# Windowed attention with relative position bias: bias products in two column halves of TensorE, spread over the heads by SBUF transfers

## The chip, the cores and the metric

The kernel runs on one NeuronCore of a Trainium2 chip. The metric is the device time of one execution in microseconds. The kernel before takes 4548.22 us, the median of 3 runs (4543.13 to 4551.57). The profile is that of one execution; its span is 4547.9 us.

Engines are called as in the profile: PE is TensorE's matmul, PEld its weight load, DVE is VectorE, ACT is ScalarE, POOL is GpSimd, SP is SyncE, which issues most of the DMAs. L383 is line 383 of the kernel.

## The reference

One layer of a metaformer on x of shape 2 x 128 x 256 x 256 (batch, channels, rows, columns), in float32. It has an attention part and a mixture of experts.

```python
# windows of 8x8 queries; each sees 12x12 keys; 4 heads of 32 channels
qkv = jnp.einsum('bchw,oc->bohw', x, W_qkv)          # x after a norm over channels
attn = jnp.einsum('bnd,bmd->bnm', q, k)              # q scaled
attn = attn + rel_pos_emb(q, rel_height, rel_width) + FIXED_MASK
attn = jax.nn.softmax(attn, axis=-1)
out = jnp.einsum('bnm,bmd->bnd', attn, v)
...                                                   # W_out, residual
# experts: top 2 of 8, on each token
router_probs = jax.nn.softmax(x @ router_w + router_b, axis=-1)
top_p, top_i = jax.lax.top_k(router_probs, K)
expert_out = jnp.einsum('bnd,edc->bnec', x, expert_w) + expert_b
```

`FIXED_MASK` leaves of the keys only those whose row and column differ from the query's by an amount of one parity. So the picture falls apart into four planes by the parity of row and column, and in each a window of 4 x 4 queries sees 6 x 6 keys. `rel_pos_emb` adds to each logit the product of the query with one vector for the difference in rows and one for the difference in columns. With 4 queries and 6 keys in a direction there are 9 possible differences: 18 products of each query and head.

The logits go through a softmax. So a number that is the same for all keys of a query may be added to its logits, and the output stays the same.

## The kernel before

It goes through 256 planes (64 strips of 8 rows, 4 planes each). A plane has 512 queries (4 rows of 128), as 32 windows of 4 columns. While TensorE works on the attention of plane n, it makes the projections of plane n + 1, and the experts' products of a row that an earlier plane has left.

The bias takes these steps. The products of queries and difference vectors are made at once from the normed input, by weights that have both matrices multiplied into each other (`wrel`): 18 rows for each head, in blocks of 32 rows.

```python
NU = 9
...
for h in range(HEADS):
    hp = slice(h * DH, (h + 1) * DH)
    for j in range(2):                      # 0: rows, 1: columns
        c0 = h * DH + NU * j
        nc.vector.tensor_copy(
            relbd[hp, c0 : c0 + NU], relT[j][hp, lo : lo + 2 * NU - 1 : 2]
        )
...
nc.tensor.matmul(pr[:, :P], lhsT=wall[:, 0, :], rhs=relbd, start=True, stop=True)
nc.vector.tensor_copy(wrel, pr[:, :P])
```

```python
def project(n, state):
    ...
    values(0)                               # L368: pvv, 4 products of 128 columns
    yield
    pu = mm_tile(f"pu{n}")
    nc.tensor.matmul(pu, lhsT=wrel, rhs=inner, start=True, stop=True)           # L383
    uT = work.tile([P, PR, 4, 32], F32, tag="uT", name=f"uT{n}", bufs=1)
    nc.vector.transpose(uT, pu.rearrange("p (a m s) -> p a s m", a=PR, s=4))    # L385
    state["shift"] = lambda: shift(uT, n, state)
    yield
    ...                                     # L395 pk (k; one product, two where a batch ends)
    ...                                     # L417 pq (q), then values(4)
```

The transpose (32 x 32 blocks) puts the differences of a query side by side. `shift` then takes, for each query, the 6 of the 9 that its position in the window needs, and transposes back:

```python
def shift(uT, n, state):
    for j in range(2):
        shifted = uT[:, :, :, NU * j + 3 : NU * j + 9]
        dims = [list(d) for d in shifted.ap]
        dims[1 + j][0] -= 1                 # one further on for each query row or column
        nc.vector.tensor_copy(              # L348
            auT[n % 2][:, :, :, 6 * j : 6 * j + 6],
            bass.AP(shifted.tensor, shifted.offset, dims),
        )
    au = work.tile([P, 2 * NP, PR, 4], F32, tag="au", name=f"au{n}")
    nc.vector.transpose(au.rearrange("p m a s -> p a s m"), auT[n % 2])         # L353
    state["au"] = au
```

`au` has, for each head, 12 rows of bias (6 for the rows of keys, 6 for the columns) in the 32 partitions of that head, and a row of -1e30 for keys that a query does not see. A product with 0/1 weights (`keys`) adds them to the logits of all keys:

```python
def scores(n, state):
    qs, kk, au = state["qs"], state["kk"], state["au"]
    ...
    for w in range(2):
        for half in range(2):
            rows = slice(half * SLOT, (half + 1) * SLOT)
            for h in range(HEADS):
                hp = slice(h * DH, (h + 1) * DH)
                nc.tensor.matmul(           # L447, tiles of 32 x 64 of the array
                    sc[rows, h].rearrange("p (t w z) -> p t w z", w=2, z=16)[:, :, w],
                    lhsT=keys[hp, turn, w],
                    rhs=au[hp, half * NP + w : (half + 1) * NP : 2].rearrange(
                        "p t a s -> p t (a s)"
                    ),
                    start=(w == 0),
                    stop=False,
                )
    ...                                     # L464: q by k, 64 products in the same tiles
```

The main loop has its order by hand; what is made on each engine stands in this order (cut):

```python
for n in range(n_planes + 7):
    ...
    if 6 <= n < n_planes:
        nc.tensor.addr_align(BLOCK, offset=BLOCK - FIRST_LIMIT)   # L786; 256, offset 161
    next(score, None)                       # bias and half of q by k
    ...
    next(score, None)                       # the rest; exp of the logits on ACT
    next(ahead, None)                       # pvv
    next(ahead, None)                       # pu
    if n + 1 < n_planes:
        states[n + 1]["shift"]()            # of the plane to come
    next(ahead, None)                       # pk
    next(ahead, None)                       # pq
    ...                                     # pg: gates to a DRAM buffer gd; rb is fetched from it
    ...                                     # four experts' products into acc (L679)
    next(norm, None)                        # squares on ACT (L541)
    next(attn, None)                        # L485 and L495: sums, attention by values
    ...                                     # fetches of gates (gb), on SP's queue; DVE: xe (L670)
    next(norm, None)                        # plt (L547, tiles of 128 x 32), lT on ACT (L555)
    ...
    next(ahead, None)                       # pvv, the other half
    ex.product(0)
    made = next(norm, None)                 # plg (L558)
    ...                                     # experts 1 to 3, po (L523)
```

`addr_align` puts NOPs into TensorE's instruction stream, as many as are needed until the next instruction stands at place 161 of a block of 256.

Of the kernel before, what the change touches and what calls it, by code (L numbers as in the profile page):

```python
# [10 lines left out]
F32 = mybir.dt.float32  # L11
AF = mybir.ActivationFunctionType
ALU = mybir.AluOpType
# [3 lines left out]
P = 128  # L17
HEADS, DH = 4, 32
# [3 lines left out]
NEG = -1e30  # L22
# [16 lines left out]

R = 8
KR, KC = 6, 10
NK = KR * KC
SLOT = 64
BLOCK, FIRST_LIMIT = 256, 95
NU = 9


@with_exitstack  # L50
def kernel(
# [16 lines left out]
    nc = tc.nc  # L68
# [25 lines left out]
    def ctile(shape, name):  # L94
        return const.tile(shape, F32, tag=name, name=name)
# [84 lines left out]
        relT.append(rT)  # L180
    mid = n_rel // 2
    lo = mid - 2 * (PR - 1)
    relbd = ctile([P, P], "relbd")
    nc.gpsimd.memset(relbd, 0.0)
    for h in range(HEADS):
        hp = slice(h * DH, (h + 1) * DH)
        for j in range(2):
            c0 = h * DH + NU * j
            nc.vector.tensor_copy(
                relbd[hp, c0 : c0 + NU], relT[j][hp, lo : lo + 2 * NU - 1 : 2]  # L190
            )
    wrel = ctile([P, P], "wrel")
    pr = mm_tile("p_wrel")
    nc.tensor.matmul(pr[:, :P], lhsT=wall[:, 0, :], rhs=relbd, start=True, stop=True)
    nc.vector.tensor_copy(wrel, pr[:, :P])

    xn, xcol, kcol = [], [], []
    for i in range(2):
# [8 lines left out]
        nc.gpsimd.memset(kcol[i][:, NP - 1, KC - 1 : NK : KC], 0.0)  # L207


    auT = []  # L210
    for i in range(2):
        auT.append(ctile([P, PR, 4, 32], f"auT{i}"))
        nc.gpsimd.memset(auT[i], 0.0)
        nc.gpsimd.memset(auT[i][:, :, :, KR + 6 : KR + 7], NEG)


    def rstd(p4, k0, k1, name):
# [123 lines left out]

    def shift(uT, n, state):

        for j in range(2):
            shifted = uT[:, :, :, NU * j + 3 : NU * j + 9]
            dims = [list(d) for d in shifted.ap]
            dims[1 + j][0] -= 1
            nc.vector.tensor_copy(  # L348
                auT[n % 2][:, :, :, 6 * j : 6 * j + 6],
                bass.AP(shifted.tensor, shifted.offset, dims),  # L350
            )
        au = work.tile([P, 2 * NP, PR, 4], F32, tag="au", name=f"au{n}")
        nc.vector.transpose(au.rearrange("p m a s -> p a s m"), auT[n % 2])  # L353
        state["au"] = au

    def project(n, state):

# [22 lines left out]


        pu = mm_tile(f"pu{n}")
        nc.tensor.matmul(pu, lhsT=wrel, rhs=inner, start=True, stop=True)  # L383
        uT = work.tile([P, PR, 4, 32], F32, tag="uT", name=f"uT{n}", bufs=1)
        nc.vector.transpose(uT, pu.rearrange("p (a m s) -> p a s m", a=PR, s=4))  # L385
        state["shift"] = lambda: shift(uT, n, state)
        yield

# [46 lines left out]
    def scores(n, state):  # L435


        qs, kk, au = state["qs"], state["kk"], state["au"]
        turn = place(n // 4, 0) // 2
        att = ps_att.tile([P, 4, 512], F32, tag="att", name=f"att{n}")  # L440
        sc = att[:, :, 0:HQ]
# [3 lines that stand above are left out]
                for h in range(HEADS):  # L445
                    hp = slice(h * DH, (h + 1) * DH)
                    nc.tensor.matmul(  # L447
                        sc[rows, h].rearrange("p (t w z) -> p t w z", w=2, z=16)[:, :, w],
                        lhsT=keys[hp, turn, w],
                        rhs=au[hp, half * NP + w : (half + 1) * NP : 2].rearrange(  # L450
                            "p t a s -> p t (a s)"
                        ),
                        start=(w == 0),
                        stop=False,
                    )
# [287 lines left out]
    for _ in project(0, states[0]):  # L743
        pass
    states[0]["shift"]()
    if n_planes > 1:
        columns(1)

# [22 lines left out]
    with tc.manual_schedule(engines={ET.PE, ET.DVE, ET.Activation, ET.Pool, ET.SP}):  # L771
        for n in range(n_planes + 7):
# [43 lines left out]
            if f or c:  # L816
                norm = norms(f, c, f"_{n}")
            next(norm, None)
            next(attn, None)
            nxt.means()  # L820
            new.fetch_means()
# [97 lines left out]
```

The softmax here doesn't subtract the row's maximum and nothing guards it: scores larger than these inputs give would overflow.

## Time and profile before

| | before |
|---|---|
| time, median of 3 runs | 4548.22 us |
| PE busy | 4490.6 us, 99% of the span |
| DVE busy | 3826.1 us, 84% |
| ACT busy | 1582.6 us, 35% |
| POOL busy | 1321.7 us, 29% |
| DMA | 824.84 MB, 181 GB/s |
| granted TensorE clock | 0.997 |

A group of instructions in the profile is a line of the kernel with an engine, an operation, and what it writes and reads: `L385 DVE STREAM_TRANSPOSE uT<-pu`. Behind it stand the count, the busy time of all in us, and the mean of one in ns. A tile of the array stands before the shape: `128*32` is 128 rows by 32 columns. Each fp32 product shows as two MATMUL records, its two passes. Matmuls are pipelined and their ends are modelled, so the distance between starts says more of them than the durations. "issue" is idle time in which the engine waited for nothing that the profile shows. The chain of work that ended last is followed back from the last instruction, at each step to what released it.

### The profile page before, as it was taken

How to read it: one execution, taken by the hardware profiler on the slowest of the kernel's cores; microseconds unless marked ns; L12 is line 12 of the kernel's file. 1: busy time of each engine (PE TensorE's matmuls, PEld its weight loads, DVE VectorE, ACT ScalarE, POOL GpSimd, SP SyncE). 2: the span in 40 equal slices, each digit the busy share in tenths (PEclk: the TensorE clock that was granted, in tenths of full speed). 3: DMA queues.
4: the chain of work that ended last, by engine and by line, in shares of the span. 5: the costliest groups of instructions: out<-in, count | busy, mean ns of one | idle time of the engine just before them, and what ended most of it. 6: DMA issues, size and time to landing. Idle time of an engine off the chain costs nothing.

```text
span 4547.9 us, 224166 instructions
## 1 busy us (share of the span) xinstructions
PE 4490.6 (99%) x96841; PEld 2708.2 (60%) x96841; DVE 3826.1 (84%) x11330; ACT 1582.6 (35%) x4542; POOL 1321.7 (29%) x1812
## 2 busy tenths in 40 slices
PE   7999999999999999999999999999999999999997
PEld 5665666565666666666666666666666656656653
DVE  5888888888888888888888888888888888888886
ACT  3333333333333333333333333333333333333331
POOL 1232323232323223232323232323232323232221
PEclk9999999999999999999999999999999999999999
DMA  2565666566556666665656665656666656666655
GB/s 76 176 191 180 190 179 191 181 190 180 189 180 189 183 186 184 186 185 183 188 181 186 183 188 181 190 180 190 180 190 180 191 179 190 182 187 181 188 163 181
DMA packets 457786, 824.84 MB, mean 181 GB/s; under 512 B 52480, under 2 KB 64356, under 8 KB 456804
## 3 DMA queue, kind: packets, MB, share of 16 engines
q1 hardware_dynamic: 456074, 810.21, 59.0%
q8 instruction: 769, 12.60, 1.1%
q14 instruction: 213, 1.74, 0.1%
q10 hardware_dynamic: 730, 0.29, 0.0%
HBM read 737.95 MB, written 72.34 MB: 178 GB/s over the span
## 4 chain that ended last, share of the span: by engine, by line
PE 97%; DVE 1%; issue 1%; DMA 0%; ACT 0%; POOL 0%; SPq 0%; ACTq 0%; DVEq 0%; POOLq 0%
PE acc L679 38%; PE pvv L368 12%; PE att L464 7%; PE att L495 6%; PE plt L547 6%; PE pu L383 5%; PE po L523 5%; PE pk L395 5%; PE pq L417 5%; PE att L447 3%; PE att L485 3%; PE pg L622 1%; PE plg L558 1%; DMA gb<-gd 0%; DVE xe L670 0%
## 5 line engine op out<-in xcount | busy, mean ns | idle before, releaser
L679 PE MATMUL acc<-xe,ew 128*128 128x512 f32 x4096 | 1921.7, 595 | 6.5 <-DVE xt L685 2.6
L679 PEld LDWEIGHTS acc<-xe,ew 128*128 128x128 f32 x4096 | 720.8, 191 | 788.1 <-issue 780.3
L670 DVE TENSOR_TENSOR xe<-xs,gb 128x512 f32<-128x512 f32 x1536 | 950.5, 686 | 10.9 <-DMA gb<-gd 2.2
L674 POOL COPY last<-xe 128x1 f32<-128x1 f32 x256 | 48.3, 189 | 3110.8 <-DVE gb L653 3103.7
L670 POOL TENSOR_TENSOR xe<-xs,gb 128x512 f32<-128x512 f32 x512 | 652.3, 1275 | 5.7 <-PE att L495 2.7
L368 PE MATMUL pvv<-wt,xcol 128*128 128x128 f32 x4096 | 595.1, 288 | 4.2 <-POOL xcol L330 3.1
L368 PEld LDWEIGHTS pvv<-wt,xcol 128*128 128x128 f32 x4096 | 497.2, 191 | 66.6 <-issue 51.9
L555 ACT COPY lT<-plt 128x128 f32<-128x128 f32 x260 | 69.3, 266 | 1141.3 <-PE plt L547 1141.3
L271 POOL TENSOR_TENSOR xn<-xt,rb 128x512 f32<-128x512 f32 x249 | 375.9, 1510 | 79.9 <-DMA rb<-gd 68.1
L464 PE MATMUL att<-qs,kcol 32*64 32x32 f32 x32768 | 391.7, 226 | 2.4 <-issue 2.4
L464 PEld LDWEIGHTS att<-qs,kcol 32*64 32x64 f32 x32768 | 390.3, 130 | 2.6 <-issue 2.6
L375 ACT COPY vv<-pvv 128x512 f32<-128x512 f32 x512 | 300.3, 586 | 207.4 <-PE pvv L368 191.4
L495 PEld LDWEIGHTS att<-pT,vv 64*32 64x32 f32 x32768 | 347.8, 105 | 36.7
L472 ACT ACTIVATE pT<-att 128x1024 f32<-128x1024 f32 x256 | 262.1, 1024 | 253.7 <-PE att L464 250.3
L495 PE MATMUL att<-pT,vv 64*32 64x32 f32 x32768 | 342.5, 200 | 0.0
L385 DVE STREAM_TRANSPOSE uT<-pu 128x512 f32<-128x512 f32 x256 | 183.5, 717 | 150.2 <-PE pu L383 150.2
L541 ACT ACTIVATE sq<-xt 128x512 f32<-128x512 f32 x505 | 292.1, 628 | 0.0
L353 DVE STREAM_TRANSPOSE au<-auT 128x512 f32<-128x512 f32 x256 | 269.2, 1051 | 9.0
L406 ACT COPY kcol<-pk 128x560 f32<-128x560 f32 (+2 forms) x344 | 174.3, 507 | 268.5 <-PE pk L395 265.7
L523 PE MATMUL po<-o,wt 128*128 128x512 f32 x512 | 261.8, 593 | 4.1 <-DVE r__0_619 L227 1.0
L383 PE MATMUL pu<-xn,wrel 128*128 128x512 f32 x512 | 263.6, 596 | 0.0
L417 PE MATMUL pq<-xn,wt 128*128 128x512 f32 x512 | 262.2, 593 | 0.5 <-issue 0.2
(2700 smaller groups left out, 5579.8 us busy)
## 6 DMA issues: line engine op xcount, KB each, us to landing
gb<-gd SPq DMA_DIRECT2D x2048, 256.0 KB
xt<-in_x_dram SPq DMA_DIRECT2D x256, 256.0 KB
sb<-gd SPq DMA_DIRECT2D x256, 256.0 KB
out_dram<-xt SPq DMA_DIRECT2D x256, 256.0 KB
rb<-gd SPq DMA_DIRECT2D x249, 256.0 KB
gd<-gT SPq DMA_DIRECT2D x245, 20.0 KB
ew<-in_L_ffn_expert_w_dram SPq DMA_DIRECT2D x1, 512.0 KB
eb<-in_L_ffn_expert_b_dram SPq DMA_DIRECT2D x1, 512.0 KB
```

The source lines that it names most:

```text
L271: eng.tensor_tensor(xn[i % 2][:, :, :, k, 1 : PC + 1], ln1_src(i, k).rearrange("p (y j x) -> p y x j", y=2, x=2), rb.rearrange("p (y j x) ...
L368: nc.tensor.matmul(pv[:, t * P : (t + 1) * P], lhsT=xl[:, t0 + t].rearrange("p a k -> p (a k)"), rhs=wv, start=True, stop=True,)
L375: nc.scalar.copy(vv[:, t0 : t0 + 4, :].rearrange("p t c -> p (t c)"), pv)
L383: nc.tensor.matmul(pu, lhsT=wrel, rhs=inner, start=True, stop=True)
L417: nc.tensor.matmul(pq, lhsT=wq, rhs=inner, start=True, stop=True)
L464: nc.tensor.matmul(sc[rows, h, 32 * t : 32 * t + 32], lhsT=kk[hp, half * HP + t, :], rhs=qs[hp, m0 : m0 + 2].rearrange("p m a s -> p (m a ...
L495: nc.tensor.matmul(av[hp, half, 32 * t : 32 * t + 32], lhsT=vv[rows, t, hp], rhs=pT[rows, h, 32 * t : 32 * t + 32], start=True, stop=True,)
L523: nc.tensor.matmul(po, lhsT=wo, rhs=state["o"].rearrange("p f z -> p (f z)"), start=True, stop=True)
L541: nc.scalar.activation(sq, src, AF.Square)
L547: nc.tensor.matmul(plt[32 * t : 32 * t + 32, :P], lhsT=rw[:, j], rhs=src[:, t * P : (t + 1) * P], start=(j == srcs[0][0]), stop=(j == srcs ...
L670: eng.tensor_tensor(self.xe[e], self.xs, self.gb.pop(e), ALU.mult)
L679: nc.tensor.matmul(self.acc, lhsT=ew[:, e, :], rhs=self.xe.pop(e), start=(e == 0), stop=not self.xe)
```

## The change

It makes the bias rows with 16 differences for each head in place of 18. The last of the 9 differences of a direction is subtracted from the other 8; that is the same number for all keys of a query, so the softmax does not see it, and the ninth difference becomes zero. Four heads of 16 rows fill 64 rows, half of the array's columns. So the plane's 512 queries are taken in two halves of 256, and each half has its own 64 columns of the array and its own 64 partitions of the result. Both products are meant to run at once. The transposes of DVE then have 256 elements in each partition in place of 512.

What comes out of DVE (`both`) has the four heads at 16 partitions each, twice. The product that adds the bias to the logits needs each head at the 32 partitions of that head. Eight transfers from SBUF to SBUF, issued by ACT, bring them there (`send`), into two buffers `au` that planes use in turn.

```diff
-    relbd = ctile([P, P], "relbd")
+    relbd = ctile([P, HEADS * NB], "relbd")          # NB = 16
...
-            c0 = h * DH + NU * j
-            nc.vector.tensor_copy(
-                relbd[hp, c0 : c0 + NU], relT[j][hp, lo : lo + 2 * NU - 1 : 2]
+            c0 = h * NB + (NU - 1) * j
+            last_d = lo + 2 * (NU - 1)
+            nc.vector.tensor_tensor(
+                relbd[hp, c0 : c0 + NU - 1],
+                relT[j][hp, lo : last_d - 1 : 2],
+                relT[j][hp, last_d : last_d + 1].broadcast_to([DH, NU - 1]),
+                ALU.subtract,
             )
...
     def shift(uT, n, state):
-        for j in range(2):
-            ...
-        au = work.tile([P, 2 * NP, PR, 4], F32, tag="au", name=f"au{n}")
-        nc.vector.transpose(au.rearrange("p m a s -> p a s m"), auT[n % 2])
-        state["au"] = au
+        to = auT[n % 2]
+        for up, (rows, start) in enumerate(((slice(0, 64), 3), (slice(64, P), 1))):
+            ...                                       # 64 partitions x 96 elements
+            nc.vector.tensor_copy(...)
+        src = uT[:, :, :, NU + 2 : NU + 8]
+        for h in range(2):
+            ...                                       # 128 partitions x 48 elements
+            nc.vector.tensor_copy(...)
+        nc.vector.memset(to[0:64, 0, :, :, 5:6], 0.0)
+        nc.vector.memset(to[:, :, 0, :, 11:12], 0.0)
+        both = work.tile([P, 2 * NP, 8], F32, tag="both", name=f"both{n}")
+        nc.vector.transpose(
+            both.rearrange("p m (a s) -> p a s m", a=2), to.rearrange("p a s h k -> p a s (h k)")
+        )
+        state["both"] = both
+
+    def send(n, state):
+        both = state.pop("both")
+        for up in range(2):
+            for h in range(HEADS):
+                r = (up * HEADS + h) * NB
+                nc.scalar.dma_start(au[n % 2][h * DH : h * DH + NB, up], both[r : r + NB])
...
         pu = mm_tile(f"pu{n}")
-        nc.tensor.matmul(pu, lhsT=wrel, rhs=inner, start=True, stop=True)
-        uT = work.tile([P, PR, 4, 32], F32, tag="uT", name=f"uT{n}", bufs=1)
-        nc.vector.transpose(uT, pu.rearrange("p (a m s) -> p a s m", a=PR, s=4))
+        for up in range(2):
+            nc.tensor.matmul(
+                pu[up * 64 : (up + 1) * 64, 0 : NQ // 2],
+                lhsT=wrel,
+                rhs=inner[:, 2 * up : 2 * up + 2],
+                start=True,
+                stop=True,
+            )
+        uT = work.tile([P, 2, 4, 32], F32, tag="uT", name=f"uT{n}", bufs=1)
+        nc.vector.transpose(uT, pu[:, 0 : NQ // 2].rearrange("p (a m s) -> p a s m", a=2, s=4))
...
-                        sc[rows, h].rearrange("p (t w z) -> p t w z", w=2, z=16)[:, :, w],
+                        sc[rows, h].rearrange("p (t w a z) -> p t w a z", w=2, a=2, z=8)[:, :, w],
                         lhsT=keys[hp, turn, w],
-                        rhs=au[hp, half * NP + w : (half + 1) * NP : 2].rearrange(
-                            "p t a s -> p t (a s)"
+                        rhs=bias[hp, :, half * NP + w : (half + 1) * NP : 2].rearrange(
+                            "p a t z -> p t a z"
                         ),
...
             next(norm, None)                          # the squares on ACT
+            if n + 1 < n_planes:
+                send(n + 1, states[n + 1])
             next(attn, None)
```

The alignment of TensorE's instructions (`BLOCK`, `FIRST_LIMIT`) stays as it was.

## The prediction

> **What bounds the kernel now.** I read the page first: the busy times, then the chain that ended last.
>
> ```profile
> PE 4490.6 (99%) x96841; PEld 2708.2 (60%) x96841; DVE 3826.1 (84%) x11330; ACT 1582.6 (35%) x4542; POOL 1321.7 (29%) x1812
> ...
> PE 97%; DVE 1%; issue 1%; DMA 0%; ACT 0%; POOL 0%; SPq 0%; ACTq 0%; DVEq 0%; POOLq 0%
> ```
>
> TensorE is busy 99% of the span and 97% of the chain is TensorE. A busy PE alone proves little, so I then read one plane of the steady part in the chain in order of time (start, length, what):
>
> ```profile
> 2011.35 0.86 PE po L523 x2
> 2012.21 0.86 PE acc L679 x2
> 2013.07 0.60 PE att L447 x30
> 2013.67 1.34 PE att L464 x80
> 2015.01 1.09 PE pvv L368 x8
> 2016.10 0.86 PE pu L383 x2
> 2016.96 0.86 PE pk L395 x2
> ```
>
> The pieces touch: no other engine is in the chain. The same piece (pk) begins at 1999.57 and at 2016.96, so a plane takes 17.39 us, and 256 planes give 4452 of the 4548 us. A microsecond of TensorE work taken from a plane is therefore worth close to a microsecond; a microsecond of DVE work is worth almost nothing. pu is one piece of 0.86 us, in two passes (x2), one for each half of the fp32 product.
>
> **What the Trainium skill says.** (1) TensorEngine Tiling (Array Packing), Key Properties: tiles of the array work in parallel, but changing the tiling mode drains TensorE. The trace agrees with both, and has the size. In the timeline of TensorE (start, us from first start to last end):
>
> ```profile
> 2006.49 0.43 PE L547 MATMUL plt<-xt,rw 128*32 128x128 f32 x8
> 2006.73 0.40 PE L547 MATMUL plt<-sq,rw 128*32 128x128 f32 x8
> 2006.95 0.40 PE L547 MATMUL plt<-xt,rw 128*32 128x128 f32 x8
> 2007.17 0.40 PE L547 MATMUL plt<-sq,rw 128*32 128x128 f32 x8
> ```
>
> Eight passes of 128 columns in four column tiles begin every 0.22 us, so 0.11 us for four tiles at once: the tiles do run together, although the two passes of one product follow each other in the program. The last eight should end streaming at 7.17 + 0.22 = 7.39, but the next piece, full-width pvv, starts at 7.50: 0.11 us of drain. Its first pass to second takes 0.21 us in the record against 0.11 for each later one: another 0.10 us, the weight load that nothing hides after a drain. Into tiles it is cheaper: the last full acc pass begins at 2012.48, streams 0.43 and ends at 2012.91, and L447 begins at 2013.00, 0.09 later; and its first group of passes takes about 0.04 longer than the rest (0.153 against 0.109).
> (2) DMA: Bandwidth & Descriptors, Anatomy of one DMA: about 2 us are fixed, mostly the receipt of the last byte. Here the 20 KB transfer gd is issued at 2019.78 and rb, which waits for it, at 2021.08: 1.3 us, to be used instead.
> (3) Runtime: NRT & Kernel Launch, Instruction fetch mechanics: instructions are fetched in blocks of 256. This kernel aligns its TensorE stream to such blocks once per plane, and the trace shows the padding as NOPs.
> (4) TensorE: Matmul & The Clock Gate, Part 1: an idle window of some 3.4 us halves the clock. No steady plane here is idle so long; it matters below.
>
> **The change part by part.**
>
> *pu.* Before, from the start of the last pvv pass to the second pass of pk: 0.112 (pvv streams) + 0.432 + 0.432 (pu) + 0.428 (pk) = 1.404 us. After, pu has two tiles of 128x64, each two passes of 256 columns. Side by side a pass is 0.215. But full-width pvv stands before it and full-width pk behind it, so there are two mode changes that were not there: 0.112 + 0.093 (drain) = 0.205; first pass 0.215 + 0.043 = 0.258; second pass and drain 0.215 + 0.113 = 0.328; first pk pass 0.428 + 0.101 = 0.529. Sum 1.320. The saving is 0.084 us, not the 0.43 that half the columns promise. Times 256: -21.5 us.
>
> *DVE.* The costs before:
>
> ```profile
> L385 DVE STREAM_TRANSPOSE uT<-pu 128x512 f32<-128x512 f32 x256 | 183.5, 717 | 150.2 <-PE pu L383 150.2
> ...
> L353 DVE STREAM_TRANSPOSE au<-auT 128x512 f32<-128x512 f32 x256 | 269.2, 1051 | 9.0
> ```
>
> Both transposes halve: about 0.38 and 0.54 us instead of 0.72 and 1.05. Two copies of 96 elements stay (0.17 each), two of 48 and two tiny memsets come (about 0.4 together). Net about -0.45 us a plane. DVE is not on the chain: 0.
>
> *The eight transfers.* In each plane ACT issues eight DMAs of 16 KB (16 rows of 1 KB). At the start of the program ACT's issues follow each other at 0.5 us (0.77, 1.26, 1.79), so eight hold its queue some 4 us. They are placed behind the two squares (last end 2003.12), and the next ACT instruction there is
>
> ```profile
> 2007.64 0.27 ACT L555 COPY lT<-plt 128x128 f32<-128x128 f32 x1 [4.52 <-PE plt L547]
> ```
>
> ACT is idle for 4.52 us before it: the issues just fit. What depends on lT, plg, comes at 2009.36 on TensorE, so lT may slip by over 1 us before TensorE waits. The last rows land some 2 us after the last issue, at about 2010, and L447 reads them at 2013.07. 128 KB more per plane against 3.2 MB (181 GB/s by 17.39 us) is 4% more traffic at 59% load. So in the steady part: hidden. Two leaks: the DMA issues of SP and ACT use eight completion semaphores in turn, so the eighth send waits until rb has landed; in the 26 planes where POOL waits for a late rb (68.1 us, of which 28.9 in one), lT may come half a microsecond too late: +5. And planes 0 to 5 take 12 to 14 us instead of 17.39 (no experts yet), so there landing after the issue is late by 1 or 2 us each: +8.
>
> *The padding.* A plane has 756 TensorE passes and loads (2 x 96841 / 256), three semaphore waits and nine NOPs: 768, three blocks. In four planes where the batch ends (k is made in two products) there are four NOPs. The padding rows, over 2234 to 2300 us and in one ordinary plane:
>
> ```profile
> L786 PEldq NOP  x16: 13/13/13, 2235.1 to 2289.2; - x16
> ```
> ```profile
> L786 PEldq NOP  x9: 13/13/13, 2411.4 to 2411.9; - x9
> ```
>
> The change adds four instructions (a second product: two loads, two passes) and waits: each head's first bias product must await two landings. One wait rides on an instruction, the other is an instruction of its own; four heads, four more. 763 + 4 = 767: ordinary planes still fit, with one NOP. The four planes at the batch's end had room for four, need eight, and are padded to 1024: 252 NOPs. A NOP looks cheap (13 ns), but 74 of them at plane 6 ran from 108.2 to 113.6 us, 0.073 us each. 252 take 18.4 us. TensorE has about 3.7 us of queued work when the padding begins (from the wait for o, about 2026.6, to L447 at 2030.39), so it stands some 14.5 us, four times: 58; with a cold clock for a while after each, 65 us.
>
> Sum: 4548 - 21.5 + 8 + 5 + 65 = 4604; I say 4600.
>
> **The rivals.** *No padding accident* (the waits count otherwise, or k's planes fit): 4548 - 21 + 13 = 4540. For it: the change leaves the alignment as it was, and my tally rests on how many waits the eight landings need. *The waits need more than five instructions:* then every plane pads to 1024 and stands 14 us, above 8000 us. Against it: a product already waits for one earlier reader, and the tally of 767 leaves one over. *Halves one after the other:* pu gains nothing and pays both mode changes, 0.35 us a plane, +88 instead of -21. Against it: plt's four tiles overlap. *The mode change is cheap for two halves:* up to 0.43 x 256 = -110, 4440. Against it: both kinds of switch show the drain. *ACT becomes the wait:* if an issue takes 0.8 us instead of 0.5, lT slips 2 us and TensorE waits about 1 us a plane, +250. Against it: the transfers have 16 rows each, fewer than those at the start.
>
> **Range and chances.** The padding accident has about 0.75 by my count, and centres on 4600; without it 4540. Eight in ten: 4530 to 4645. Faster by over 2% (below 4457) needs the drains to vanish: 0.03. Slower by over 2% (above 4639) needs serial halves, a blocked ACT or padding everywhere: 0.18. Within 2%: 0.79.
>
> **What would show it.** pu as 128*64, 128x256, four records a plane, two starts within 0.01 us; about 0.2 us of idle in all around pu; pk's first pass longer by 0.1; the plane at 17.30 us. DVE busy lower by about 110 us. ACT's eight issues between the squares and lT, lT still just after plt. Four planes near 2235 to 2310 with some 250 NOPs and 30 us each, all others with one. I am wrong if planes 128 to 131 are as long as others, if the steady plane is not shorter by 0.05 to 0.12 us, or if L447 waits for a landing in the steady part.

## The result and the profile after

A plane is counted from its first bias product (L447 before, L488 after) to that of the next one. An ordinary plane is one from 6 to 247 outside the four at the batch's end. A bracket behind a ratio is its 95% interval.

| | before | after |
|---|---|---|
| time, median | 4546.16 us | 4919.62 us (4916.77 to 4928.26) |
| ratio | | 1.0823 [1.0805, 1.0842] |
| ordinary plane, median | 17.405 us | 18.585 us |
| ordinary plane, mean | 17.429 us | 18.559 us |
| start to the first L447 or L488 | 31.54 us | 33.19 us |
| planes 0 to 5 together | 82.14 us | 100.69 us |
| four planes at the batch's end | 71.6 us | 141.4 us |
| from plane 248 on | 214.7 us | 223.4 us |

The change costs 8.2% where 1% was predicted. The rows add up: 238 ordinary planes by 1.13 us (mean) are 269, the four planes 70, the start 1.7 + 18.6, the end 9, together 368 us; the two profiled spans differ by 4916.3 - 4547.9 = 368.4 us. The four planes were in the prediction. The 1.13 us in every ordinary plane was not.

The page of the changed kernel, busy times and chain by engine:

```profile
PE 4603.8 (94%) x97353; PEld 2739.2 (56%) x97353; DVE 3695.0 (75%) x12354; ACT 1580.1 (32%) x4542; POOL 1330.3 (27%) x1814
...
PE 92%; issue 6%; DVE 1%; DMA 1%; ACTq 1%; ACT 0%; POOL 0%; SPq 0%; DVEq 0%; POOLq 0%
```

TensorE still makes the chain, but 6% of it is now "issue": TensorE stood and waited for nothing that the profile names. And PE's busy time rose by 113 us although the change takes work from it. Both have to be found. The chain in order of time (start, length, what), one plane:

```profile
2010.62 0.61 PE att L488 x30
2011.23 1.34 PE att L505 x80
2012.57 1.09 PE pvv L402 x8
2013.65 0.58 PE pu L418 x4
2014.24 0.63 PE pk L436
2014.87 0.45 issue
2015.31 0.70 PE pk L436
...
2020.99 1.49 PE att L536 x78
...
2023.49 1.09 PE pvv L402 x8
...
2028.98 0.60 PE att L488 x30
```

Two pieces differ from the plane of before. pk is cut in two with a hole between its passes, and the product of probabilities and values (L536, before L495; called the dense block below) takes 1.49 us; before it began at 2005.22 and the product after it at 2006.49. Over all planes, from start to start, the second pass of pk comes 1482 ns after the first (median; before 428), and the 128 passes of L536 take 1384 ns from first to last (before 1145). With pu and the weight load it shows, the way from the last pvv pass to the second pass of pk is 0.205 + 0.274 + 0.309 + 1.482 = 2.270 us against 1.404, +0.87; L536 has +0.24; together 1.11 of the 1.13.

The groups of the changed kernel (busy in us, mean ns of one, idle before and what ended it) that answer to those shown of before:

```profile
L488 PE MATMUL att<-au,keys 32*64 32x128 f32 x8192 | 184.0, 284 | 63.5 <-issue 60.9 <-DMA au<-both 2.4
...
L377 DVE STREAM_TRANSPOSE both<-auT 128x256 f32<-128x256 f32 x256 | 164.7, 643 | 27.2 <-DVE auT L375 8.2
L426 DVE STREAM_TRANSPOSE uT<-pu 128x256 f32<-128x256 f32 x256 | 115.2, 450 | 166.2 <-PE pu L418 166.2
...
L599 PE MATMUL plg<-ident,lT 128*128 128x128 f32 x260 | 71.4, 275 | 13.5 <-ACT lT L596 13.5
```

The last of them in the kernel before:

```profile
L558 PE MATMUL plg<-ident,lT 128*128 128x128 f32 x260 | 70.9, 273 | 0.0
```

The transposes have shrunk from 717 to 450 and from 1051 to 643 ns. TensorE waited 2.4 us in the whole run for a landing in au, and 13.5 us for lT (before none), all of it in planes 0 to 5. So in the steady part hardly anything waits for the transfers. They hurt in another way, below.

### The profile page after: what moved, and what is told of

It is laid out like the page before. It is cut to its first block, busy times and chain, and to the rows that moved or that the text cites. A ratio compares the mean times of both kernels' runs of the same rounds, so it can differ in the third digit from the quotient of the medians.

```text
span 4916.3 us, 228790 instructions
## 1 busy us (share of the span) xinstructions
PE 4603.8 (94%) x97353; PEld 2739.2 (56%) x97353; DVE 3695.0 (75%) x12354; ACT 1580.1 (32%) x4542; POOL 1330.3 (27%) x1814
## 4 chain that ended last, share of the span: by engine, by line
PE 92%; issue 6%; DVE 1%; DMA 1%; ACTq 1%; ACT 0%; POOL 0%; SPq 0%; DVEq 0%; POOLq 0%
PE acc L720 35%; PE pvv L402 11%; PE att L505 7%; PE att L536 7%; PE pk L436 7%; PE plt L588 5%; PE po L564 4%; PE pq L458 4%; PE att L488 3%; PE pu L418 3%; PE att L526 3%; PE pg L663 1%; PE plg L599 1%; ACTq L388 1%; DMA gb<-gd 0%
## 5 line engine op out<-in xcount | busy, mean ns | idle before, releaser
L436 PE MATMUL pk<-xn,wt 128*128 128x512 f32 (+2 forms) x528 | 356.2, 684 | 186.7 <-issue 186.7
L546 DVE STREAM_TRANSPOSE sT<-att 128x512 f32<-128x512 f32 x256 | 183.5, 717 | 377.8 <-PE att L536 377.8
L536 PEld LDWEIGHTS att<-pT,vv 64*32 64x32 f32 x32768 | 394.7, 105 | 52.7 <-issue 3.2
L536 PE MATMUL att<-pT,vv 64*32 64x32 f32 x32768 | 402.7, 200 | 2.9 <-issue 2.8
L505 PE MATMUL att<-qs,kcol 32*64 32x32 f32 x32768 | 397.0, 227 | 6.5 <-issue 6.5
L505 PEld LDWEIGHTS att<-qs,kcol 32*64 32x64 f32 x32768 | 395.8, 131 | 6.9 <-issue 6.9
L447 ACT COPY kcol<-pk 128x560 f32<-128x560 f32 (+2 forms) x344 | 174.1, 506 | 506.2 <-PE pk L436 502.5
L436 PEld LDWEIGHTS pk<-xn,wt 128*128 128x128 f32 x528 | 98.7, 189 | 415.4 <-issue 320.9
L569 DVE TENSOR_TENSOR xt<-po,xt 128x512 f32<-128x512 f32 x256 | 177.1, 692 | 125.1 <-PE po L564 125.0
L628 ACT ACTIVATE lg<-lg 128x32 f32<-128x32 f32 x256 | 58.7, 229 | 659.2 <-DVE lg L627 659.2
```

Source lines behind the costliest of these rows:

```text
L436: nc.tensor.matmul(pk[:, : m * PC], lhsT=wk, rhs=xp[:, part[0] : part[0] + m, 1 : PC + 1], start=True, stop=True,)
L505: nc.tensor.matmul(sc[rows, h, 32 * t : 32 * t + 32], lhsT=kk[hp, half * HP + t, :], rhs=qs[hp, m0 : m0 + 2].rearrange("p m a s -> p (m a ...
L536: nc.tensor.matmul(av[hp, half, 32 * t : 32 * t + 32], lhsT=vv[rows, t, hp], rhs=pT[rows, h, 32 * t : 32 * t + 32], start=True, stop=True,)
```

## The experiments

The base of a run is the kernel before or the changed kernel; an edit stands on its own. A few fixes stay in as the series goes on, and each says from which run it starts. Times are medians; the kernel before was timed beside each group, at 4543 to 4550 us.

### 1. Where the end of an instruction block falls

The prediction counted how many instructions a plane has, and not which instruction stands at a block's end. In the compiled stream of TensorE, counted, the end of the second block of a plane falls before instruction 351. In the kernel before that is the first of the expert products (acc), with pu, pk, pq and pg in front of it. In the changed kernel the plane has eight more instructions by there (four waits in L488, four for pu), and number 351 is the weight load of pk's second pass. The Trainium skill, Runtime: NRT & Kernel Launch, Instruction fetch mechanics, says that crossing to the next block is "mostly hidden". Two runs move the block's end alone.

b_fl87, the kernel before with its block's end moved eight instructions, onto pk:

```diff
-BLOCK, FIRST_LIMIT = 256, 95
+BLOCK, FIRST_LIMIT = 256, 87
```

> The kernel before with nothing changed but the place of its TensorE instructions in the fetch blocks: 8 slots on, so that a block ends between the two passes of pk, where it ends in the changed kernel. Theory (the block's end costs the time): pk's second pass starts about 1.4 us after its first instead of 0.43, L495 takes some 0.2 us longer, the plane goes from 17.40 to about 18.5 us and the whole to about 4830 us. Rival (the time comes from the transfers, ACT or the tiling mode): nothing of that is in this kernel, so it stays at 4546 us.

Measured: 4764.72 us, ratio 1.0486 [1.047, 1.0502]: nothing of the change is in this kernel, and it loses 219 us. The chain:

```profile
2019.67 0.86 PE pu L383 x2
2020.54 0.43 PE pk L395
2020.96 0.89 issue
2021.85 0.70 PE pk L395
2022.55 0.86 PE pq L417 x2
```

The hole stands where it stands after, between the two passes of pk; from pass to pass it is 1288 ns (median). Here the crossing is not hidden. L495 kept its 1146 ns: the part of the expectation that had the second loss from the block's end as well is refuted.

a_fl103, the changed kernel with the block's end back before acc:

```diff
-BLOCK, FIRST_LIMIT = 256, 95
+BLOCK, FIRST_LIMIT = 256, 103
```

> The changed kernel with the alignment moved by 8 slots, so that the blocks end before the same instructions as in the kernel before (the first of the experts' products, and the 208th of L536). Theory: the steady plane falls from 18.58 to 17.31 us (the 0.084 us of pu gained), the four padded planes (66 us) and the first planes (20 us) stay, the whole is about 4612 us. Rival: still about 4900 us.

Measured: 4698.17 us, 1.0332 [1.0317, 1.0348]; a plane takes 17.654 us.

```profile
2026.66 0.58 PE pu L418 x4
2027.24 1.06 PE pk L436 x2
2028.30 0.86 PE pq L458 x2
```

pk is one piece again, 534 ns from pass to pass, which is the 0.529 of the prediction. Of the 1.13 us a plane, the block's end is thus 0.95 (1482 - 534 ns), the largest term of the whole result. But the total stayed 86 us above what was expected, as L536 did not recover: 1482 ns. So L536 has a cause of its own.

The traces also have the fetches: packets of 16 KB on the DMA queue q8, three a plane. Of each ordinary plane, the first of them, and what follows it (medians in us, the lowest in brackets):

| run | fetch starts after the plane's start | second pass of pk after the fetch's start | first acc after the fetch's start |
|---|---|---|---|
| before | 2.87 | 1.36 | 2.76 (2.20) |
| a_fl103 | 2.84 | 1.31 | 2.71 (2.20) |
| after | 2.75 | **2.35** (2.17) | 3.85 |
| b_fl87 | 2.74 | **2.36** (2.17) | 3.86 |

The change does not move the fetch. Where pk's second pass stands first in the new block, it comes some 2.35 us after the fetch's start and never under 2.17, although the time from pass to pass goes from 0.9 to 1.9 us in nine planes of ten (after). By the work alone it would come 1.3 us after it, and acc 2.7. That this fetch brings the block that is waited for is inferred from these times.

### 2. The four padded planes

a_fix: from a_fl103, the alignment is left out for planes 128 to 131. The limits are set so that the blocks end before acc in the planes after these; in planes 6 to 127 they end sixteen instructions later, behind the first eight acc passes.

```diff
-BLOCK, FIRST_LIMIT = 256, 95
+BLOCK, FIRST_LIMIT = 256, 119
...
-            if 6 <= n < n_planes:
-                nc.tensor.addr_align(BLOCK, offset=BLOCK - FIRST_LIMIT)
+            if 6 <= n < n_planes and not 128 <= n < 132:
+                limit = FIRST_LIMIT if n < 128 else FIRST_LIMIT - 16
+                nc.tensor.addr_align(BLOCK, offset=BLOCK - limit)
```

> As a_fl103, but around the end of the batch the alignment is left out for four planes, and the places before and after differ by the 16 slots that those planes add, so no plane is padded to a fourth block. Theory: the four planes lose their 15 to 17 us each: about 4546 us, 66 us below a_fl103. If the padding is not what holds them, no difference.

Measured: 4636.4 us, 1.0198 [1.0183, 1.0213]; the four planes take 17.8 to 17.9 us each, 69 us less together than in a_fl103. The total fell by 62 us only, because the new limit pads elsewhere: 254 NOPs stand ahead of plane 6, from 130.7 to 149.5 us, where a_fl103 has 14, and planes 0 to 5 take 115.9 us in place of 98.9. In the changed kernel the rows of the padding (count, first and last start) show the ordinary planes with one NOP, 18.6 us apart, and one of the four with its many:

```profile
L828 PEldq NOP  x2: 13/13/13, 2211.2 to 2229.8; - x2
```
```profile
L828 PEldq NOP  x206: 13/13/13, 2400.0 to 2415.2; - x103
```

and its chain shows what they cost, 12.87 us of issue before L488:

```profile
2402.48 12.87 issue
2415.35 1.27 PE att L488 x22
```

In the 14.65 us behind it the granted clock was 0.84, and the products took longer (L488 1.27 us in place of 0.61).

### 3. The second loss: what slows L536

nosend_fl99: the changed kernel without its eight transfers, block's end before acc. The scores then lack nearly all of the bias.

```diff
-BLOCK, FIRST_LIMIT = 256, 95
+BLOCK, FIRST_LIMIT = 256, 99
...
-                nc.scalar.dma_start(au[n % 2][h * DH : h * DH + NB, up], both[r : r + NB])
+                pass
```

> As a_fl103, but the eight transfers are left out, so the bias is missing from the logits and the output is not the reference's; TensorE loses four waits, so the alignment is set to bring the blocks' ends to the same instructions. Theory (the transfers are hidden in the steady part): the plane is the same as in a_fl103 within 0.05 us; the four planes fit their three blocks again and the first planes lose the wait, so about 4525 us. Rival (the transfers hold ACT or the DMA queues): the steady plane is shorter than that of a_fl103 by 0.2 us or more.

Measured: 4522.4 us, 0.995 [0.9934, 0.9967]; L536 1145 ns, a plane 17.304 us. The rest of the change brings what the prediction gave it: 17.405 - 0.084 = 17.32. The transfers cost some 0.33 us a plane (a_fix against this run), and 0.31 of it lies in L536.

Within L536 of a_fl103 the loss is not spread. From pass to pass TensorE keeps its pace, with single stops in between, mostly of 75 to 180 ns. Of 396 stops over 60 ns in 245 planes (one of 0.11 us near the block's start, which the kernel before has too, is not counted), 386 begin 150 to 300 ns after an issue of a transfer by ACT began. The issues follow each other every 0.64 us, so this does not tell the start of one from the end of the one before. Is it the bytes, the time, or the place in the stream?

a_fix2_tiny: from a_fix, 32 bytes of each row in place of 1 KB (most of the bias is left out).

```diff
-                nc.scalar.dma_start(au[n % 2][h * DH : h * DH + NB, up], both[r : r + NB])
+                nc.scalar.dma_start(au[n % 2][h * DH : h * DH + NB, up, 0:1], both[r : r + NB, 0:1])
```

> Block ends as in the run a_fix (4636 us, L536 from first to last start 1455 ns); each of the 64 rows-by-halves transfers of a plane stays, but carries 8 elements of a row (32 bytes) in place of 256 (1 KB), so 4 KB a plane in place of 128 KB; most of the bias is left out, so the output is not the reference's. If the bytes that the transfers move through SBUF slow L536: L536 back to about 1150 ns and the total about 4560 us. If it is the eight issues, their descriptors and their semaphores: L536 stays at 1350 to 1480 ns and the total is 4610 to 4640 us. Waits of lT for the transfers get shorter in both cases and bring nothing to the total.

Measured: 4637.5 us, 1.0192 [1.0177, 1.0207], L536 1469 ns, as a_fix. A transfer of 512 bytes stops TensorE as long as one of 16 KB. It isn't the bytes; the number of rows, 16, was the same. (The expectation's count of 64 transfers a plane is a slip: it is eight.)

a_fix2_late: from a_fix, `send` is called after `lT` and the next load of x, and the scores read the other buffer (the bias of another plane).

```diff
-        qs, kk, bias = state["qs"], state["kk"], au[n % 2]
+        qs, kk, bias = state["qs"], state["kk"], au[(n + 1) % 2]
...
-            if n + 1 < n_planes:
-                send(n + 1, states[n + 1])
             next(attn, None)
...
             load_x((n + 9) // 4, (n + 9) % 4, paced=True)
+            if n + 1 < n_planes:
+                send(n + 1, states[n + 1])
```

> Block ends as in the run a_fix; the eight sends are issued by ScalarE after the probability transposes of the plane instead of before L536, and the scores read the other bias buffer, so that nothing waits for them sooner than they land (the bias of another plane is added, so the output is not the reference's). If L536 is slow only because the sends run beside it: L536 at about 1150 ns and, with nothing else slowed, a plane of 17.30 us and a total of about 4550 us. If any sends of the plane slow whatever TensorE does meanwhile: the 0.3 us turns up in another block (L488 or the gate's matmuls) and the total stays at 4620 to 4640 us. If L536 is slow from its place in the stream and not from the sends: L536 stays at 1455 ns.

Measured: 5167.65 us, 1.1356 [1.1336, 1.1375]. L536 is at 1145 ns, so the time at which the transfers run decides. But the gain is more than lost elsewhere, which no theory had. From the waits (us in total, times, longest):

```profile
ACT vv L409 <- DMA au<-both: 1712.9, 253, 9.8
```

There ACT stands at its issues for 6.8 us a plane, and the copies of vv, kcol and qs behind them are late for TensorE.

a_fix2_pufirst: from a_fix, pu is made before the first pvv, directly behind L505, which works in parts of the array too. Then one change of mode is saved.

```diff
-        values(0)
-        yield
         pu = mm_tile(f"pu{n}")
...
         state["shift"] = lambda: shift(uT, n, state)
         yield
+        values(0)
+        yield
```

> Block ends as in a_fix; pu is made before the first pvv instead of after it, so the two-halves products stand behind other matmuls that also use part of the array, and one change of mode with its weight load in the open (205 ns from pvv to pu in the changed kernel) is saved; the sends come about 1 us sooner. If the drain is saved: 0.1 to 0.2 us a plane, total 4590 to 4615 us, L536 unchanged at about 1450 ns or a little shorter. If the change of mode costs the same in the new place: within 5 us of a_fix's 4636 us. If the earlier sends leave L536 in part: below 4580 us.

Measured: 4585.53 us, 1.0081 [1.0064, 1.0097]; a plane takes 17.475 us, 0.157 less than in a_fix (medians; 0.126 in the mean), L536 1455 ns. Another 18 us came in planes 0 to 5 and the start: 2 NOPs stand ahead of plane 6 in place of a_fix's 254. Without that the total would lie in the range expected.

a_fix2_split: from a_fix2_pufirst, four of the eight issues go to SP, directly after the copies.

```diff
                 states[n + 1]["shift"]()
+                send(n + 1, states[n + 1], (0,), nc.sync)
...
-                send(n + 1, states[n + 1])
+                send(n + 1, states[n + 1], (1,))
```

> As a_fix2_pufirst, but the four transfers of the first half are issued by SyncE directly after the copies, and only four are left to ScalarE at the old place. If the sends slow L536 by running beside it: fewer run beside it, L536 falls to 1150 to 1300 ns and the total to 4500 to 4570 us. If the number of transfers or their bytes in a plane counts and not when they run: the total stays within 10 us of a_fix2_pufirst. Against both: SyncE's four issues may hold back the loads that it issues next, and then the waits of L488 for its experts' inputs would grow.

Measured: 4805.83 us, 1.0565 [1.0549, 1.0581]. L536 (here L534) is at 1358 ns, but the point named against both came true: SP's four issues took 3.15 us (median), its load of the gate's rows began 11.9 us after the plane's start in place of 7.9, and the work on the normalised x came late, and pq with it. From the waits:

```profile
POOL xn L284 <- DMA rb<-gd: 744.5, 243, 37.8
PEld pq L456 <- DVE uT L421: 369.4, 242, 2.4
```

### 4. The disputed cost by itself

Four runs on the kernel before, each with eight transfers a plane of 16 rows by 512 bytes that nobody reads, at the place where the change has its `send`. Only the two ends and the issuing queue differ.

```diff
             next(norm, None)
+            for up in range(2):                                        # b_sends
+                for h in range(HEADS):
+                    r = (up * HEADS + h) * 16
+                    nc.scalar.dma_start(dump[n % 2][h * DH : h * DH + 16, up], ident[r : r + 16])
```

b_dram reads `c_keys[r : r + 16, 0]` in DRAM in place of `ident`; b_sp has `nc.sync` in place of `nc.scalar`; b_store writes 16 rows of `ident` to a tile in DRAM.

> The kernel before, unchanged but for eight transfers a plane that nobody reads: ScalarE issues, at the place where the changed kernel has its sends, eight copies of 16 rows of 512 bytes of a constant tile into a scratch tile. PE's stream stays at 759 instructions. If each issue by ScalarE that falls beside L495 stops TensorE for 0.10 to 0.17 us, about two a plane: L495 from 1145 ns to 1400 to 1480 ns, nothing else of TensorE changed, a plane from 17.40 to 17.65 to 17.75 us, total 4605 to 4630 us. If L536's slowing came from anything else of the change (the place of the block's end, waits for au or both, the order of work on VectorE): L495 stays at 1145 ns and the total within 10 us of 4546 us.

> As b_sends (4631 us, L497 1428 ns, 1.7 stalls a plane), but the eight unread transfers take their 512-byte rows from DRAM instead of SBUF; ScalarE issues them at the same place. If ScalarE's issue beside the dense block is what stops TensorE: L497 again 1380 to 1460 ns and the total 4610 to 4640 us. If it is the reading of SBUF by transfers: L497 at 1145 ns and the total at 4540 to 4560 us.

> As b_sends, but SyncE issues the eight unread transfers from SBUF, at the same place of the program. If any queue's transfers from SBUF to SBUF stop TensorE: L497 at 1300 to 1460 ns, with stalls that begin 150 to 300 ns after an issue by SyncE. If only ScalarE's issues do: L497 at 1145 ns, no stalls. The total tells little here, as SyncE's loads of the experts' gates stand behind the eight: 4560 to 4800 us in either case.

> As b_sends (4631 us, L497 1428 ns) and b_dram (4560 us, 1145 ns), but the eight unread transfers, 16 rows of 512 bytes each, go from SBUF to DRAM. If the reading of SBUF is what stops TensorE: the dense block at 1300 to 1460 ns and the total 4590 to 4635 us. If it takes a transfer from SBUF to SBUF: the block at 1145 ns and the total at 4540 to 4565 us.

| run | from, to, issued by | time, us | ratio | dense block, ns |
|---|---|---|---|---|
| b_sends | SBUF to SBUF, ACT | 4630.88 | 1.0199 [1.0183, 1.0215] | 1428 |
| b_sp | SBUF to SBUF, SP | 4969.32 | 1.0928 [1.091, 1.0946] | 1474 |
| b_dram | DRAM to SBUF, ACT | 4560.38 | 1.0032 [1.0019, 1.0045] | 1145 |
| b_store | SBUF to DRAM, ACT | 4571.81 | 1.0045 [1.0028, 1.0061] | 1146 |

b_sends repeats the second loss without anything else of the change: 0.28 us in each plane's dense block against 0.31 in a_fix. (That both totals are 2.0% above is chance: a_fix also has the gain of pu and the padding ahead of plane 6.) Its timeline (start, length, what), the issues of ACT and the dense block (the product of L495):

```profile
2028.51 3.81 ACTq L824 DMA_DIRECT2D dump<-ident  x6
...
2030.75 1.67 PE L497 MATMUL att<-pT,vv 64*32 64x32 f32 x128
```

The same in b_dram:

```profile
2028.11 2.32 ACTq L824 DMA_DIRECT2D dump<-in_c_keys_dram  x5
...
2029.47 1.34 PE L497 MATMUL att<-pT,vv 64*32 64x32 f32 x128
```

In both, issues run on beside the block; only in b_sends is the block longer. It isn't the issue by ACT, as the block of b_sp is slow too. And it isn't the reading of SBUF alone, as b_store is not slow: the first theory of b_dram's expectation and of b_store's falls, and what is left is a transfer with both ends in SBUF. The dose shows it plane by plane. Counted in planes 10 to 254 are the transfers whose issue ended inside the block, up to 0.28 us before its last pass starts, and beside them the block's median length in ns (planes in brackets; three planes of gap4 with three transfers are left out):

| run | 0 | 1 | 2 |
|---|---|---|---|
| b_sends | | 1301 (78) | 1484 (167) |
| b_sp | | 1309 (68) | 1502 (177) |
| a_fix2_tiny | | 1306 (64) | 1492 (181) |
| gap4 (below) | 1145 (117) | 1331 (104) | 1510 (21) |
| b_dram | | 1145 (58) | 1145 (187) |
| b_store | 1146 (2) | 1146 (59) | 1146 (184) |

A transfer from SBUF to SBUF costs the block 0.16 to 0.19 us, a second one as much again; to or from DRAM nothing. Why TensorE stops is not shown. The Trainium skill, SBUF — State Buffer, SBUF: two separate sides, says that accesses of engines and of transfers to SBUF do not get in each other's way; b_dram and b_store agree; the stops of b_sends do not fit it, unless they come about outside SBUF, which no run here tells.

The total of b_sp is above its range, and most of it is something else, a hole before acc:

```profile
PE acc L681 <- issue: 263.9, 240, 2.6
```

It looks like the block's end of part 1. The fetch starts 4.38 us after the plane's start there, in place of 2.87, and acc comes 2.39 us after the fetch's start (medians). Why the fetch starts later is not shown. The 14 and 22 us that b_dram and b_store lose are not in the block; planes 0 to 5 have 4.6 and 8.5 of them.

### 5. Getting the transfers out of the way

gap5 and gap4: from a_fix2_pufirst, ACT issues the first five (or four) before its squares, and SP the rest between its store of the gate's rows and the load of them.

```diff
         nc.sync.dma_start(gd[lo:hi], gT[: hi - lo])
+        then()              # send(n + 1, states[n + 1], PARTS[5:], nc.sync)
...
+            if n + 1 < n_planes:
+                send(n + 1, states[n + 1], PARTS[:5], nc.scalar)
             if f or c:
                 norm = norms(f, c, f"_{n}")
             next(norm, None)
-            if n + 1 < n_planes:
-                send(n + 1, states[n + 1])
```

> As a_fix2_pufirst (4585 us), but three of the eight transfers are issued by SyncE between its store of the gate's rows and its load of them back, where it waits some 1.7 us, and five by ScalarE, before its two squares instead of after them. All eight are then issued before L536 begins. If an issue beside L536 is what stops TensorE: L536 back to 1150 to 1200 ns, a plane at 17.15 to 17.25 us and the total at 4505 to 4530 us, below the kernel before. If the landing of the transfers and not their issue does it: L536 at 1300 ns or more and the total above 4550 us. Against both: if SyncE's three issues wait for slots, the load back comes later, and GpSimd's and the gate's waits grow as in a_fix2_split (4806 us).

> As gap5 with four and four: ScalarE is done 0.6 us sooner, SyncE's load back of the gate's rows comes 0.3 to 0.6 us later. By the issue theory L536 is at 1145 ns and the total within 10 us of gap5's; if SyncE's load back is what counts, it is above gap5 by 0.1 us or more a plane, 25 us or more.

Measured: gap5 4558.14 us, 1.0034 [1.0022, 1.0047]; gap4 4579.17 us, 1.0083 [1.0069, 1.0096]. In gap5 the branch came true that names the landing and not the issue: the block has 1332 ns (gap4 1209) and the total is above 4550 us. The traces say the same. Of 294 stops over 60 ns in the two runs, 277 begin 190 to 350 ns after an issue has ended, and only 24 while one runs. So it is not the issue beside the block that stops TensorE, but the transfer that it has set off. The issues end 0.9 and 0.6 times a plane inside the block, in a_fix2_pufirst 1.7 times. In gap4 the block gained less than SP's later load cost (GpSimd waited 416.8 us for it, in gap5 342.6).

thru_dram: from a_fix2_pufirst, the spreading goes through DRAM, one store of all of `both` before the squares and four loads after them. (The scores wait less often then, so the plane has four instructions less. The limit moves to 115, where the blocks end behind the first eight acc passes, and needs no other value for later planes; planes 128 to 131 go without alignment, as in a_fix.)

```diff
+    def put(n, state):
+        bd = dram.tile([P, 2 * NP, 8], F32, tag="bd", name=f"bd{n}")
+        nc.scalar.dma_start(bd, state.pop("both"))
+        state["bd"] = bd
+
     def send(n, state):
-        both = state.pop("both")
-        for up in range(2):
-            for h in range(HEADS):
-                r = (up * HEADS + h) * NB
-                nc.scalar.dma_start(au[n % 2][h * DH : h * DH + NB, up], both[r : r + NB])
+        bd = state.pop("bd").rearrange("(u r) m z -> r u m z", u=2)
+        for h in range(HEADS):
+            nc.scalar.dma_start(au[n % 2][h * DH : h * DH + NB], bd[h * NB : (h + 1) * NB])
```

> As a_fix2_pufirst (4585 us, L534 1455 ns), but the spreading goes through DRAM: one transfer stores the whole of both, issued before ScalarE's two squares, and four transfers, one a head with both halves, bring it into au, issued after the squares. So one transfer a plane reads SBUF, some 3 us before the dense block, and none beside it; TensorE's stream has 763 instructions a plane, as the scores wait for au less often. If transfers that read SBUF are what stops TensorE: L534 at 1145 ns, no stalls, a plane at 17.15 to 17.25 us, and the total at 4500 to 4530 us, below the kernel before. If transfers into au stop it as well (their writes, or their issue): L534 at 1300 ns or more and the total above 4555 us. Against both: ScalarE may wait for the store to land before it issues the loads, which the gate's waits for lT would show.

Measured: 4495.22 us (4488.72 to 4496.56), 0.9889 [0.9872, 0.9905]: faster than both kernels, and a little below the range expected. Its timeline, with the store, the loads and the dense block, which some of the loads run beside:

```profile
2017.70 0.34 ACTq L385 DMA_DIRECT2D bd<-both  x1
2020.57 1.75 ACTq L392 DMA_DIRECT2D au<-bd  x4
2021.32 1.34 PE L538 MATMUL att<-pT,vv 64*32 64x32 f32 x128
```

and its page:

```profile
PE 4426.0 (99%) x97353; PEld 2666.4 (59%) x97353; DVE 3731.7 (83%) x12354; ACT 1582.5 (35%) x4542; POOL 1325.2 (30%) x1814
...
PE 96%; DVE 2%; issue 1%; DMA 1%; ACT 0%; ACTq 0%; POOL 0%; SPq 0%; DVEq 0%; POOLq 0%
```

The block has 1145 ns in planes with no, one or two loads beside it, "issue" is back to 1%, and a plane takes 17.110 us. That is 0.295 less than before: of it 0.08 is what a_fl103 shows for pu, 0.157 what a_fix2_pufirst shows for its new place, and 0.05 is not assigned.

## The prediction, step by step

**Right: pu.** From the last pvv pass to pk's second, a_fl103 has 0.205 + 0.274 + 0.309 + 0.534 = 1.322 us; 1.320 was predicted. The two halves start 7 ns apart. The cost of a mode change, read from neighbouring products, carried over to a place where none had been.

**Right: VectorE.** Its busy time fell by 131 us (110 predicted). Two misses cancel in it: the transposes shrank to 450 and 643 ns, not to 380 and 540, and the copies and memsets added 0.16 us a plane, not 0.4. No gain of it is to be seen: nosend_fl99, which has all of it, gained 0.10 us a plane, and pu alone explains 0.08.

**Right: the padding, as far as it was counted.** One NOP stands in ordinary planes and 252 in each of four, which take some 35 us each, 70 us more in all than before. The prediction had 58, or 65 with a cold clock. The stand before L488 was 12.9 us in place of 14.5, and the slower clock behind it took part of the rest.

**Wrong: the padding, in what it left out.** The step "763 + 4 = 767: ordinary planes still fit, with one NOP" took a fitting number for a harmless one. Eight more instructions ahead of it moved the block's end from acc onto pk's second weight load, which by the work alone comes 1.3 us after the fetch's start, while the block's first instruction waits until 2.35 us after it. That is 0.95 us a plane (a_fl103), and b_fl87 shows nearly as much, 0.86, in the kernel before without the change. The prediction had looked at the NOPs, which the trace names; the place of a block's end has to be counted, and held against the packets of q8.

**Wrong: "So in the steady part: hidden".** The transfers were hidden from everything that waits for them: ACT issues them before lT, and TensorE waits 2.4 us in a whole run for au. They were not hidden from a product that has nothing to do with them. Transfers from SBUF to SBUF that run beside L536 stop TensorE, some 1.6 to 1.75 times a plane, 0.15 to 0.19 us for each: 0.24 us in the changed kernel, 0.31 with the block's end moved (a_fix), 0.28 in the kernel before (b_sends). None of the rivals had it. The argument from bytes (4% more traffic) asked the wrong question: the bytes do not matter (a_fix2_tiny).

**The two leaks: one too large, one too small and with another cause.** The late lT in steady planes, +5, did not come: TensorE's six waits for lT, 13.5 us, lie in planes 0 to 5, one in each. There the loss was 18.6 us instead of 8, although fewer NOPs stand ahead of plane 6 (22 in place of 74). The prediction's cause for it, late landings, has 2.4 us of waits; most of it is lT, behind ACT's issues. An issue follows the one before after 0.64 us in place of 0.5, so eight hold ACT's queue 5.1 us. In b_sends, where nobody waits for a transfer, the same planes lose 10.6 us.

**The rivals.** Serial halves, a cheap mode change and padding in every plane are refuted by the records of pu and of the NOPs; ACT as the wait by the waits for lT, of which the steady planes have none. *No padding accident* is refuted by the four planes of 35 us.

## What to carry to other kernels

When a change adds or moves instructions ahead of an aligned block's end, find the instruction that stands there, and in the DMA packets the fetch that goes before it. Here an instruction that was due 2.7 us after the fetch's start lost nothing, and one that was due after 1.3 us lost 0.95 us in every plane. Then count the NOPs of the whole run again, as a new limit can pad in another place (a_fix, plane 6). A transfer that nobody waits for is not free: see what TensorE runs beside it, and keep transfers from SBUF to SBUF away from a block like the dense one here, or send them through DRAM. A result that contradicts a sum is best met by giving the suspected piece to the kernel before, alone.

## What the runs showed of the hardware

- A transfer of 16 rows from SBUF to SBUF stops TensorE by 0.16 to 0.19 us in a block where passes follow each other every 8.4 ns (67 ns for eight), 190 to 350 ns after its issue has ended; 512 bytes do it as 16 KB do, from ACT's queue and from SP's (b_sends, b_sp, a_fix2_tiny, gap4, gap5). To DRAM or from it there is no stop (b_store, b_dram, thru_dram).
- Such an issue also holds ACT's queue longer: six take 3.81 us in b_sends, 0.63 each; four loads from DRAM take 1.75 us in thru_dram, 0.44 each.
- What stands first in a fetch block came no sooner than 2.17 us after the fetch's first packet, with holes at a median of 2.35 us (after), 2.36 (b_fl87) and 2.39 (b_sp). Where the work alone takes longer, as up to acc (2.76 us before), the fetch costs nothing; between the passes of pk it made 1288 ns of 428 (b_fl87) and 1482 of 534 (after).
- ACT stands at an issue, with all that is behind it, when an earlier transfer has not landed: 1712.9 us in a_fix2_late, where the issues were meant to be out of the way.
